# Attention over 16 batches: the large heads' probabilities transposed on VectorE and moved by transfers, five weights reloaded per batch

## The chip, the core and the metric

The kernel runs on one core of a Trainium2 chip. The metric is the device time of one execution in microseconds (us). The engines are TensorE (PE, with its weight loads PEld), VectorE (DVE), ScalarE (ACT), GpSimd (POOL) and SyncE (SP), which here only issues transfers.

## The reference, cut to what matters

Four cross-attention layers follow each other for 16 batches. `x` is (16, 100, 256) and the context is (16, 361, 256). All are float32, and every layer has 16 heads. Layers 0 and 3 have heads of 16 columns ("small heads"), layers 1 and 2 have heads of 64 columns ("large heads").

```python
# layer 0: layer norm of query and context, heads of 16, then a feed-forward block
scores = einsum('bqhd,bkhd->bhqk', Q, K) / sqrt(16)
x = residual + softmax(scores) @ V @ wo + bo
x = x + gelu(layer_norm(x) @ w1 + b1) @ w2 + b2
# layer 1: root-mean-square norm of the query, heads of 64, no scale
x = x + softmax(q @ k.T) @ v @ wo
# layer 2: heads of 64, rotary embedding of q and k, scale 1/8, mask, layer norm at the end
scores = where(mask, rope(q) @ rope(k).T / 8, -1e9)
x = layer_norm(x + softmax(scores) @ v @ Wo)
# layer 3: layer norms, heads of 16, biases, residual
```

The weighted sum of one head contracts over the 361 keys, so the probabilities, which leave the softmax with the 100 queries on the partitions, must be turned so that the keys lie on the partitions.

## The kernel before

The program is written out as a list of works (`Plan.add`, L263): each names the engines that can run it, its reads, writes and buffers. `Plan.order` (L304) replays the list with estimated durations, chooses an engine and a buffer slot for each work, and gives the final order of instructions on every engine. The ranks in `ORDER` (`lag`, `place`, `ends`) are constants that shift this choice. On the chip every engine then runs its instructions in that order, and waits on semaphores where a work reads what another engine or a transfer writes. Two batches at a time are in flight, with buffers of their own (`p = b % 2`); the loop over the 16 batches is `for b in range(B): batch(b)` (L1443).

All weights are kept on the chip: twelve slabs of 128x2048 float32 (1 MB each) are loaded once at the start (`load_slab`). After that SP issues only the batch's context, query rows and mask, and the store of the result.

An attention layer (`Attention`, L904) goes through four units (`unit`, L922), each of four heads. For one unit:

- `scores` (L933): TensorE multiplies queries and keys into one PSUM bank per head, 361 keys in two parts of 181 and 180. The large heads take 64 rows of the array each, so that two heads run side by side.
- `exponential` (L975): VectorE negates the scores and takes their maximum in one pass (L991); with a mask, in layer 2, it takes the minimum with the cap (L985) and then the maximum (L988). ScalarE takes the exponential with the sum of the row (L997).
- `softmax` (L953): VectorE inverts the sums (L961), GpSimd divides (L968).
- `transposed` (L1011): TensorE transposes the probabilities of two heads by 12 instructions (L1032): for each head and each of three chunks of 128 keys, 64 queries and 36 queries at two places of the array. The results lie in PSUM, and ScalarE or VectorE copies them to `pT` in three copies per unit (`copied`, L711 and L713). There are two `pT` buffers.
- `weighted` (L1052): TensorE multiplies `v` and `pT` (through `on_columns`, L830), chunk by chunk of the keys.

`values` (L1300) computes `v` of half of the large heads at a time, with the keys of chunk `j` on the partitions. `rotated` (L874) applies the rotary embedding of layer 2: VectorE swaps neighbouring rows out of PSUM (`stream_shuffle`, L885), GpSimd multiplies by the sine (L889), VectorE multiplies PSUM by the cosine (L892), and GpSimd adds both (L897). `feed_forward` (L1339) uses `w1` and `w2`, `project_out_T` (L1124) an output weight. `by_parity` (L1202) spreads the small heads' queries over two copies, on VectorE.

TensorE runs in tiling modes (`row64` for transposes and large scores, `row32` for small scores, `col32` for all projections and weighted sums), and the plan groups works of one mode.

Of the kernel before, what the change touches and what calls it, by code (L numbers as in the profile page):

```python
# [17 lines left out]
P = 128  # L18
# [6 lines left out]
SKP = NKC * KP  # L25
BIG = 3.0e38
# [5 lines left out]
for _name, _w in (  # L32
# [10 lines left out]

SLABS = (
# [12 lines left out]
    "lag": 281400, "pull": 6.35, "window": 0,  # L57
    "keep": {None: 4180, "row64": 280, "row32": 710, "col64": 3610, "col32": 5250},
    "run": {None: 3260, "row64": 33260, "row32": 18740, "col64": 46890, "col32": 300},
    "batch": (-614500, -19500, 0, 0, 0, 0, 0, 0, 0, 0, 0, 0, 0, 0, 6000, -863500),  # L60
    "place": [
        100 * k for k in (
        1530, 2179, 1302, -155, -3146, -3119, -1447, -50, 2198, -4316, -4647, -2582, -7311,
        -6990, -6791, -975, -6218, -4297, -1712, -7295, -4489, -3822, -7130, -4520, -2986,
        -5107, -1814, 2539, -585, 44, -2295, -3865, -3674, -5144, -5622, -10071, -9468, -6347,
        -6509, -5109, -6468, -10008, -6583, -10112, -6656, -7056, -6274, -9553, -10961, -12648,
        -6592, -6491, -10074, -11842, -5012, -7475, -5864, -2138, -2644, -2757, -1752, -1661,
        -3175, -1806, -475, 295, -1528, -1314, -130, -2596, -3455, -3510, -486, 819, -960, -351,
        -262, -1091, -2095, 773, 352, 609, -2745, -1077, -4127, -3906, 1115, -1980, -1044, 199,
        1113, -2251, -559, -4303, 204, 507, -7028, -6650, -4569, -6483, -2121, -3493, -985,  # L70
        -4030, 928, 291, -3776, -3852, -4367, -2262, -3068, -1405, 3055, -1796, -1471, -2884,
        -3509, -3745, -408, -473, -4075, -5224, -5147, -1610, -3815, -3333, -4064, -6731, -5900,
        -7478, -6211, -2778, -3243, -2860, 346, 2670, -1934, 358, -4143, -3642, -2093, -2165,
        -529, 13, -685, -1077, -415, 5064, -896, -533, -6410, 8, -1286, 795, -1181, 3287, 2325,
        1250, 437, 2327, 2459, -1757, -1578, -5694, -990, 2513, 7808, 7794, 4228, 183, 3326,
        3721, 2104, 3855, 1016, 3932, -5255, -932, -801, -1656, 458, -71, 3547, -2879, -7942,
        1183, -679, -3284, -3147, -4837, -4906, -3658, -1029, -5460, -1795, -2290, -3716, -633,
        -1243, 250, 3042, 115, 3644, 209, 517, 802, 3561, 2033, 8348, 2938, -2370, -768, 91,
        -3053, -3682, 21, -551, -703, 11, -1354, -76, -6811, -5354, -5457, -3261, -4456, -5041,
        -4118, -7857, -5743, -9610, -9289, -7014, -6103, -6155, -5974, -3208, -5827, -5655,  # L80
        -3748, -6019, 1222, -6204, 1169, 1555, 804, 4287, 847, 1540, 2681, 4086, 3349, 8301,
        3405, 2300, 1930, -158, 2379, 3910, 4211, 3253, -272, -266, -2428, -1347, 2024, 88,
        -3112, -7985, -3868, 994, 1277, -1300, -464, -390, 2333, 3472, 2811, 3971, 4406, 6487,
        7550, 8667, 4711, 4737, 1877, 3779, 2319, 8022, 4465, 4476, 4993, 5707, 6778, 4543,
        5848, 4450, 5898, 5280, 5713, 2599, 4430, 8324, 4133, 8528, 6706, 596, 2298, -498, -905,
        1966, -4295, -1105, -3795, -5564, -1315, 1532, -3363, -2789, -552, 18, -3105, -6266,
        -10045, 1320, -6270, -4428, -689, -4740, -3580, 963, -5363, -2314, 1942, 5363, 3756,
        3169, 735, -4085, 2025, 1750, 1971, 2138, 2974, 3519, 5203, 5507, -452, 3042, -190, 412,
        -928, -229, 3162, -526, 895, -1352, -1376, -3942, -3984, -379, -7134, -2812, 551, -6423,
        -2341, -2152, -3333, 1507, -1188, 1764, 4650, 1708, -78, 1087, 3668, 2857, -1320, -858,  # L90
        -553, -1310, -4001, -416, -2796, -2804, -3944, -3808, -3234, -2595, -5780, -8117, -7507,
        -10136, -9612, -9238, -7690, -3249, -4884, -5928, -7611, -6301, -4692, -3495, -11110,
        -9091, -6761, -5493, -6295, -1317, -740, 731, -2244, -69, -536, 1225, -1389, -3686,
        -3052, 1470, -6939, -3363, -3396, -8455, -10700, -13129, -12689, -11245, -7208, -10167,
        -10536, -5830, -7870, -7456, -6041, -4659, -7272, -4839, -3132, -1617, -5559, -2862,
        1514, 625, -188, 1018, -3554, -7159, -3278, -5544, -4708, -2643, -3131, -6058, -6394,
        1652, -6383, 298, -1138, -636, 2469, 408, -1417, 3200, 3186, 3478, 1178, 3587, 3199,
        6766, 4361, -6638, -2795, -3377, -7601, -7151, -544, 106, 696, 3907, 4138, 174, -2346,
        -2919, -5554, -4166, -6125, -7266, -5804, -4121, -1761, -2439, -2442, -6500, -2289,
        -5069, -2101, -1548, -4952, -9599, -7022, -7908, -8951, -3814, -1275, 1254, 521, 1148,  # L100
        2417, 2197, 5182, 1520, 1334, -2249, -1420, -3655, 2699, 1623, 5275, 3648, 4868, 2758,
        2532, -689, 507, -519, 767, 6121, 2545, 1546, 1364, 5831, 5011, 3375, 4931, 2510, 1069,
        -2819, -2364, -1352, 736, 211, 7491, 5251, 3010, 3340, -1837, -316, -4152, -1590, -7796,
        -2636, -2985, -4463, -3344, -3607, -3647, -175, 99, 2885, 1406, -3051,
        )
    ],
    "ends": {
        0: (
            -360, -553, -1511, 2397, 964, 789, -725, 912, 2373, -371, 41, 464, 1613, 1142, 2683,
            1305, 1591, 1084, 1716, 523, 2216, 90, -1353, -388, -1656, -1072, -274, -339, -11,  # L110
            155, 632, -171, 502, -673, -1637, -182, 1897, 672, 1857, -596, -378, -333, 1238,
            2379, 469, 1904, -164, 63, -794, 573, 808, -1509, -1850, -1626, -1597, -3151, -3544,
            -2672, -900, -1650, -798, -2350, -1910, -1679, -1847, -698, -2383, -2743, -5180,
            -4612, -2344, -2016, -1852, -3270, -1884, 112, 362, -992, -1005, 724, 1778, 650,
            2305, 599, 2425, 619, 1458, 3273, 1790, 4855, 2263, 3341, 5414, 1727, 1515, 3046,
            1719, 1836, 3007, 3679, 2096, 2898, 5452, 3383, 5487, 2059, 2757, 3025, 3143, 6789,
            5244, 6917, 4771, 5135, 4386, 3985, 5106, 4688, 5087, 4942, 4236, 3046, 2670, 2706,
            3503, 2091, 1847, 3076, 2014, 1388, 1104, 1622, 656, -58, -699, -1176, 358, 1608,
            650, 1589, 2114, 1883, 2341, 2921, 2511, 3381, 3691, 4413, 3140, 4228, 2483, 3948,
            2043, 2066, 931, 1432, 1360, 1782, -86, -18, 837, -930, -270, -363, 814, 2353, 1627,  # L120
            643, -38, -161, -146, -1206, -375, -3069, -315, -3728, -3105, -3361, -2754, -3800,
            -1483, -3606, -4088, -5311, -4059, -5705, -6399, -5862, -6911, -5959, -5318, -4142,
            -5855, -4077, -6440, -6281, -5759, -5040, -4004, -6200, -4200, -5136, -4332, -4595,
            -3567, -4424, -2153, -3404, -4608, -3125, -3018, -1565, -4138, -1906, -3823, -2916,
            -4261, -4211, -4430, -4353, -4078, -4346, -2581, -1226, -3347, -414, -1217, -70,
            352, -362, 2766, 1590, 2947, 76, 1035, 1343, 2115, 230, 1068, 914, 987, 299, 1055,
            684, -333, -908, -1103, 180, 966, 2428, 1138, 3173, 2381, 3194, 2268, 2281, 4818,
            2345, 3968, 2898, 2699, 4290, 3602, 3022, 1639, 2723, 1823, 1069, 1598, 615, 1470,
            1948, 1732, 1430, 1545, 3316, 3001, 2864, 1194, 2011, 1984, 1999, 2991, 940, 1758,
            492, 994, -419, 2734, 3609, -90, 190, 731, 2958, 562, 689, 1347, 969, -80, 453, 154,  # L130
            56, -1037, 348, -1744, 43, 860, -1679, 219, -1277, -405, -1163, 609, -392, -842,
            664, -1860, -2046, -2459, -1830, -3185, -2962, -3331, -4173, -2284, -952, -420,
            -2511, -2702, -1827, 984, -629, -2108, -2626, -2178, 617, -343, -442, -299, 2765,
            1451, 1872, 3147, 1723, 1384, 657, 2253, 2961, 4622, 1312, 1265, 3200, 448, 335,
            974, 1119, 332, 1507, -455, -919, 902, 3211, 2790, 2410, 3753, 1212, 3920, 2793,
# [57 lines left out]
        ),  # L193
    },
}

class Buf:
# [209 lines left out]
def tile_xattn_layers(  # L409
# [147 lines left out]
    for i in (2, 3, 6):  # L557
        load_slab(i)
# [939 lines left out]
```

## Time and profile before

| | |
|---|---|
| median of 2 runs | 1936.38 us (1935.73 to 1937.03) |
| span of the profiled execution | 1935.2 us |
| mean granted TensorE clock | 0.993 |
| TensorE busy | 1914.6 us (99%) |
| VectorE busy | 1294.5 us (67%) |
| ScalarE busy | 1170.2 us (60%) |
| GpSimd busy | 1045.9 us (54%) |
| TensorE transposes of the probabilities (L1032) | 6144, 240.8 us busy |
| transfers | 29.94 MB, 15 GB/s over the span |

The profile is of one execution, and its span is 1.2 us below the median of the runs. "Busy" is the time in which at least one instruction of the group was running. TensorE's instructions overlap, so a group's mean duration is far above the time that one more instruction adds. The mean of the transposes is 226 ns, while 24 of them take 0.89 us from the first start to the next work's start. The granted clock is the share of full speed that TensorE was given.

### The profile page before, as it was taken

The numbers are of one execution on the slowest core, as the hardware profiler recorded it, in microseconds if no ns is written. First come the engines' busy times: TensorE is split into PE (matmuls) and PEld (weight loads), VectorE is DVE, ScalarE is ACT, GpSimd is POOL, SyncE is SP. The second block draws the span as 40 slices with busy tenths as digits, with TensorE's granted clock in tenths as the row PEclk, the third lists the DMA queues.
The fourth block names the chain that finished last, engine by engine and source line by source line (L and its number), as shares of the span: only waits on it lengthen the run. The fifth ranks groups of instructions, "written<-read, shape, count | busy, mean of one in ns | idle before, by whom it ended". The sixth has DMA issues, their size and how long they took to land.

```text
span 1935.2 us, 99776 instructions
## 1 busy us (share of the span) xinstructions
PE 1914.6 (99%) x43881; PEld 1268.0 (66%) x43881; DVE 1294.5 (67%) x4502; ACT 1170.2 (60%) x3418; POOL 1045.9 (54%) x1682
## 2 busy tenths in 40 slices
PE   8999999999999999999999999999999999999997
PEld 4667666575766757667575675766657576575766
DVE  5556676766667666666666676667676667765776
ACT  4646556575665746657566565665657566575645
POOL 5355465555556555555645555556555555654564
PEclk9999999999999999999999999999999999999997
DMA  7000000000000000000000000000000000000000
GB/s 305 3 3 14 5 12 8 3 14 5 12 8 3 14 5 12 8 3 15 5 14 6 11 9 3 14 5 12 8 3 14 6 12 8 3 15 5 3 3 7
DMA packets 14730, 29.94 MB, mean 15 GB/s; under 512 B 3362, under 2 KB 12376, under 8 KB 12888
## 3 DMA queue, kind: packets, MB, share of 16 engines
q1 hardware_dynamic: 14296, 23.56, 3.8%
q8 instruction: 344, 5.64, 1.2%
q14 instruction: 90, 0.74, 0.1%
HBM read 21.92 MB, written 1.64 MB: 12 GB/s over the span
## 4 chain that ended last, share of the span: by engine, by line
PE 97%; DVE 1%; POOL 1%; ACT 0%; issue 0%; DMA 0%; SPq 0%; POOLq 0%; DVEq 0%; ACTq 0%
PE ps L830 70%; PE ps L936 14%; PE ps L1032 11%; PE ps L771 1%; PE ps L858 1%; PE ps L813 0%; ACT prob L997 0%; DMA slab<-slabs_dram 0%; DVE prob L991 0%; PE ps L616 0%; PE ps L665 0%; POOL prob L968 0%; DVE pT L713 0%; DVE prob L985 0%; POOL kT L897 0%
## 5 line engine op out<-in xcount | busy, mean ns | idle before, releaser
L968 POOL TENSOR_SCALAR prob<-prob,two 100x361 f32<-100x361 f32 x1024 | 566.2, 571 | 551.6 <-DVE two L961 335.2
L997 ACT ACTIVATE prob<-prob,two 100x361 f32<-100x361 f32 x1024 | 602.0, 592 | 138.6 <-DVE prob L991 87.2
L991 DVE TENSOR_SCALAR_CACHE_REDUCE prob<-ps 100x361 f32<-100x361 f32 x768 | 372.3, 530 | 143.7 <-PE ps L936 126.7
L830 PE MATMUL ps<-slab,cT 128*32 128x512 f32 (+1 forms) x3072 | 367.0, 595 | 0.0
L830 PE MATMUL ps<-cT,slab 128*32 128x361 f32 x4096 | 346.0, 468 | 0.0
L936 PE MATMUL ps<-kT,qT 32*100 32x181 f32 (+3 forms) x4096 | 303.3, 328 | 2.9 <-DVE qT L1204 1.4
L711 ACT COPY pT<-ps 128x384 f32<-128x384 f32 (+1 forms) x521 | 231.1, 492 | 93.4 <-PE ps L1032 77.4
L936 PEld LDWEIGHTS ps<-kT,qT 32*100 32x100 f32 (+1 forms) x4096 | 228.1, 164 | 74.8 <-issue 30.8
L1032 PEld LDWEIGHTS ps<-ident,prob 36*128 36x128 f32 (+1 forms) x6144 | 215.3, 140 | 85.1 <-POOL prob L968 62.8
L1032 PE MATMUL ps<-ident,prob 64*128 64x64 f32 (+1 forms) x6144 | 240.8, 227 | 1.5 <-ACT pT L711 0.8
L713 DVE COPY pT<-ps 128x384 f32<-128x384 f32 (+1 forms) x247 | 137.4, 573 | 130.9 <-PE ps L1032 128.7
L711 ACT COPY v<-ps 128x512 f32<-128x512 f32 (+1 forms) x119 | 69.7, 586 | 245.6 <-PE ps L830 161.8
L830 PEld LDWEIGHTS ps<-cT,slab 128*32 128x32 f32 x4096 | 123.1, 109 | 134.7 <-issue 122.4
L997 ACT ACTIVATION_READ_ACCUMULATOR prob<-prob,two 100x1 f32 x1024 | 194.0, 189 | 0.0
L889 POOL TENSOR_TENSOR sw<-sw,rot 128x361 f32<-128x361 f32 x128 | 105.3, 824 | 135.6 <-DVE sw L885 110.2
L830 PEld LDWEIGHTS ps<-slab,cT 128*32 128x32 f32 (+1 forms) x3072 | 85.3, 107 | 139.2 <-issue 127.3
L985 DVE TENSOR_TENSOR prob<-ps,cap 100x361 f32<-100x361 f32 x256 | 125.5, 527 | 62.6 <-PE ps L936 37.9
L830 PE MATMUL ps<-pT,v 128*32 128x100 f32 (+1 forms) x6144 | 155.3, 250 | 0.3 <-ACT pT L711 0.3
L830 PEld LDWEIGHTS ps<-pT,v 128*32 128x32 f32 (+1 forms) x6144 | 136.0, 110 | 22.7 <-issue 13.2
L897 POOL TENSOR_TENSOR kT<-kT,sw 128x361 f32<-128x361 f32 x128 | 122.5, 959 | 5.7
L988 DVE TENSOR_REDUCE two<-prob 100x1 f32<-100x361 f32 x256 | 125.6, 517 | 0.0
L830 PE MATMUL ps<-xT,slab 128*32 128x100 f32 x5120 | 124.1, 252 | 1.1 <-ACT xT L791 1.1
(105 smaller groups left out, 2329.6 us busy)
## 6 DMA issues: line engine op xcount, KB each, us to landing
slab<-slabs_dram SPq DMA_DIRECT2D x11, 1024.0 KB
ctxr<-ctx_dram SPq DMA_DIRECT2D x16, 256.0 KB
ctxr<-ctx_dram SPq DMA_DIRECT2D x16, 105.0 KB
x<-x_dram SPq DMA_DIRECT2D x16, 100.0 KB
out_dram<-x SPq DMA_DIRECT2D x16, 100.0 KB
slab<-slabs_dram SPq DMA_DIRECT2D x2, 512.0 KB
mask<-mask_dram SPq DMA_DIRECT2D x16, 45.1 KB
rows<-rowvecs_dram SPq DMA_DIRECT2D x1, 640.0 KB
```

The costliest lines, as they stand in the source:

```text
L711: nc.scalar.copy(dst(), src())
L713: nc.vector.tensor_copy(dst(), src())
L830: nc.tensor.matmul(out_f(at + t, at + t1), lhsT=lhsT[:, t:t1], rhs=rhs, start=start, stop=stop, tile_position=(0, at + t),)
L889: nc.gpsimd.tensor_tensor(a, a, wide(sin()), ALU.mult)
L897: nc.gpsimd.tensor_tensor(dst_f(dst.ap), dst_f(dst.ap), sw.ap[:, :n], ALU.add)
L936: nc.tensor.matmul(banks[h].ap[:S, k0:k1], lhsT=self.q_of(h), rhs=self.k_of(h)[:, k0:k1], start=(k0 == 0), stop=(k1 == SK), skip_group_che ...
L968: nc.gpsimd.tensor_scalar(p.ap[:S, :SK], p.ap[:S, :SK], rsum.ap[:S, j : j + 1], 1.0, ALU.mult, ALU.mult,)
L985: nc.vector.tensor_tensor(p(), bank.ap[:S, :SK], self.cap.ap[:S, :], ALU.min)
L988: nc.vector.tensor_reduce(neg_max.ap[:S, 0:1], p(), AX.X, ALU.max, negate=True)
L991: nc.vector.tensor_scalar(p(), bank.ap[:S, :SK], -1.0, None, ALU.mult, ALU.min, accum_out=neg_max.ap[:S, 0:1],)
L997: nc.scalar.activation(p(), p(), AF.Exp, bias=neg_max.ap[:S, 0:1], scale=1.0 if masked else -1.0, accum_out=sums.ap[:S, j : j + 1],)
L1032: nc.tensor.transpose(out[:, c, :], probs[h].ap[q0:q1, c * KP : (c + 1) * KP], ident[q0:q1, q0:q1],)
```

## The change

For the large heads alone, TensorE no longer transposes the probabilities. Queries are laid out in four blocks of 32 columns, of which 25 hold queries and seven stay zero (`QN`, `BLK`, `spread`, `split`), so that the scores of a large head have 128 rows. The new `exchanged` replaces `transposed`: for each pair of heads one VectorE instruction transposes all 32x32 blocks of the probabilities (128x768) into `blocks`. The keys of a block are then on the 32 partitions of the query block's quadrant. Sixteen transfers per unit, issued by SP, take each quadrant's blocks to the quadrant of `pT` that the weighted sum needs, in runs of 1536 bytes per partition. There are three `blocks` buffers and three `pT` buffers; the small heads still go through `transposed` and share `pT`. `values` puts the keys on the partitions in the matching order, and the weighted sum reads its 100 query columns as four runs of 25.

To make room, five weights (`STREAMED`) are no longer kept: `stream` loads each of them again for each batch into one of two `ring` buffers. The large heads' `v` has three buffers in place of two for each parity of the batch.

In `rotated`, the product with the cosine moves to GpSimd, after a copy out of PSUM by ScalarE or VectorE. `by_parity` can also run on ScalarE. Two memsets of `qT` are added at the start. All constants of `ORDER` are different, so the order of the works differs on every engine.

```diff
-        "prob": slots_of("prob", 8, [P, SKP]),
-        "pT": slots_of("pT", 2, [P, 4, NKC, S]),
+        "prob": slots_of("prob", 4, [P, 2, SKP]),
+        "blocks": slots_of("blocks", 3, [P, 4, NKC, 4 * BLK]),
+        "pT": slots_of("pT", 3, [P, NKC * NQ * 4 * BLK]),
+
+        "v": slots_of("v", 3, [P, NKC, 512]),
+        "ring": slots_of("ring", 2, [P, 2048]),
...
     for p in range(2):
+        nc.gpsimd.memset(slots[f"qT{p}"][0], 0.0)
...
+    def stream(name, b, begun):
+
+        t = plan.buf("ring", f"{name}_{b}")
+        i = SLABS.index((name,))
+
+        def issue(_):
+            nc.sync.dma_start(out=t.ap, in_=slabs[i])
+
+        return t, plan.add([("SP", 450.0, 7000.0)], issue, writes=[t], begun=begun)
...
         def times_cos(_):
-            nc.vector.tensor_tensor(
-                shaped(dst_f(dst.ap)), shaped(ps.ap[:, :n]), wide(cos()), ALU.mult
-            )
+            a = into()
+            nc.gpsimd.tensor_tensor(a, a, wide(cos()), ALU.mult)
...
         plan.add(on_dve(n + 20), swap, reads=[ps], writes=[sw])
         plan.add(on_pool(2.3 * n), times_sin, reads=[sw, rot], writes=[sw])
-        plan.add(on_dve(n), times_cos, reads=[ps, rot], writes=[dst])
+        copied(into, lambda: shaped(ps.ap[:, :n]), n, [ps], [dst])
+        plan.add(on_pool(2.5 * n), times_cos, reads=[dst, rot], writes=[dst])
         plan.add(on_pool(2.5 * n), both, reads=[sw, dst], writes=[dst])
...
+            self.rows = P if hd == 64 else S
...
-                                banks[h].ap[:S, k0:k1], lhsT=self.q_of(h),
+                                banks[h].ap[: self.rows, k0:k1], lhsT=self.q_of(h),
...
+            turned = self.exchanged if hd == 64 else self.transposed
+            self.weighted(i, groups, heads, turned(probs, heads, f"{name}_{i}"))
...
+        def exchanged(self, probs, heads, name):
+
+
+            blocks, pT = plan.buf("blocks", f"{name}_blocks"), plan.buf("pT", f"{name}_pT")
+            made = []
+            for u, (prob, parts) in enumerate(probs):
+                made.append(plan.buf(None, f"{name}_made{u}"))
+
+                def transpose(_, u=u, prob=prob):
+                    to = blocks.ap[:, :, :, 2 * u * BLK : 2 * (u + 1) * BLK].rearrange(
+                        "p b c (h q) -> p h (b c) q", h=2
+                    )
+                    nc.vector.transpose(to, prob.ap.rearrange("p h (b q) -> p h b q", q=BLK))
+
+                plan.add(
+                    [("DVE", 870.0, 955.0)], transpose, reads=[prob, *parts], writes=[made[u]],
+                    takes=[blocks],
+                )
+
+            def p_of(h, c, n):
+                a = pT.ap.rearrange("p (j c h q) -> p j c h q", c=NKC, j=NQ, h=4)
+                return a[:n, :, c, heads.index(h), :QN]
+
+            def move(_):
+                for j in range(NQ):
+                    for b in range(4):
+                        n = NKC * 4 * BLK
+                        nc.sync.dma_start(
+                            out=pT.ap[b * BLK : (b + 1) * BLK, j * n : (j + 1) * n],
+                            in_=blocks.ap[j * BLK : (j + 1) * BLK, b].rearrange("p c n -> p (c n)"),
+                        )
+
+            plan.add([("SP", 5600.0, 8000.0)], move, reads=[blocks, *made], writes=[pT])
+            return pT, p_of
...
+        o_buf, _ = stream(wo, b, begun=[att.first[2]])
+        return project_out_T(att.oT, 8, wo, o_buf, resid, p, f"L{L}_x_{b}"), att
+
+    def feed_forward(b, xt, gate):
         p = b % 2
+        w1_buf, loaded = stream("L0_xattn_w1", b, begun=[gate])
+        w2_buf, _ = stream("L0_xattn_w2", b, begun=[loaded])
...
+        q_buf, _ = stream("L2_xattn_Wq", b, begun=[att.first[3]])
```

## The prediction

> **What bounds the kernel now.** I read the page first: busy time by engine, then the chain that ended last.
>
> ```profile
> PE 1914.6 (99%) x43881; PEld 1268.0 (66%) x43881; DVE 1294.5 (67%) x4502; ACT 1170.2 (60%) x3418; POOL 1045.9 (54%) x1682
> PE 97%; DVE 1%; POOL 1%; ACT 0%; issue 0%; DMA 0%; SPq 0%; POOLq 0%; DVEq 0%; ACTq 0%
> q1 hardware_dynamic: 14296, 23.56, 3.8%
> ```
>
> TensorE is busy for 99% of the span and holds 97% of the chain; the next engine, VectorE, is at 67%, and the transfers are almost idle. Work taken off TensorE is time, as long as nothing new makes it wait. Next the groups by shape, and the chain in order of time for one stretch (start, duration, what):
>
> ```profile
> L1032 PE MATMUL ps<-ident,prob 64*128 64x64 f32 x3072 | 240.8, 226 | 1.5 <-ACT pT L711 0.8 <-POOL prob L968 0.2
> L885 DVE STREAM_SHUFFLE sw<-ps 128x361 f32<-128x361 f32 x128 | 73.5, 575 | 0.6 <-issue 0.4
> L885 DVE STREAM_SHUFFLE sw<-ps 128x400 f32<-128x400 f32 x32 | 19.6, 614 | 0.0
> L892 DVE TENSOR_TENSOR kT<-ps,rot 128x361 f32<-128x361 f32 x128 | 66.9, 524 | 9.8 <-PE ps L830 9.1 <-PE ps L813 0.7
> 908.12 0.89 PE ps L1032 x23
> ```
>
> One unit of four heads costs TensorE 0.89 us for its transposes, first start to the next work's start. Last, the timeline of the transfer queue (start, duration, instruction), and two stretches of the table by windows (length, busy times PE to POOL, granted clock, DMA share, GB/s):
>
> ```profile
> 21.16 4.38 SPq L517 DMA_DIRECT2D slab<-slabs_dram  x5
> 300.42 0.30 SPq L494 DMA_DIRECT2D x<-x_dram  x1
> 331.51 0.30 SPq L1436 DMA_DIRECT2D out_dram<-x  x1
> 32.00:36.00 4.00, 4.00 (x104) 2.87 (x100) 1.74 (x4) 2.96 (x8) 3.84 (x7) 1.00 1.02 426
> 1900.00:1908.00 8.00, 4.04 (x78) 3.02 (x82) 6.14 (x28) 5.47 (x18) 4.47 (x8) 0.70 0.00 0
> ```
>
> An ordinary issue takes 0.30 us of the queue, five large ones in a row 0.88 us each. With all transfer engines busy at 426 GB/s, TensorE was busy throughout at full clock, so transfers as such do not slow it. Where it waits, the clock falls (0.70 at the end).
>
> **The change part by part.**
>
> *Transposes off TensorE.* 2 large layers x 16 batches x 4 units = 128 units; in the listing 3072 of 6144 transposes are gone. 128 x 0.89 = 113.9 us by the chain; starts to next starts over all 6144 (222.3 us) give 111.2, half of the group's busy time 120.4. I take **-111**. The other TensorE work keeps its count. Changes between tiling modes go from 823 to 790, which I count as nothing.
>
> *Wider scores.* Large heads load 128 columns of queries instead of 100. Weight loads of the same two passes took 90 ns with 9 columns and 109 with 32, 0.83 ns a column: 28 columns are 23 ns, over 2048 loads, two at a time, 24 us if nothing hid it. Loads overlap the 181-column matmul before (329 ns): I take 0, bounds 0 to 24. The weighted sum reads the same 100 columns in runs of 25; broken runs have no row. Rows of 100 unbroken columns lie between 249 and 255 ns; 2% of its 140 us is 3. I take 0.
>
> *VectorE.* Added: 256 block transposes of 128x768. No row; nearest are the shuffles: 39 more elements cost 39 ns, so 614 + 368 x 1.0 = 982 ns; by proportion 1223 ns. I take 0.98: +251 us (upper end 313). Lower end: 768 elements at half the shuffle's slope plus its 214 ns, 0.60 us. Removed by the listing: 109 copies to pT (62 us), the 160 products of L892 (85), 89 query scalings (28), and some copies shift between engines. VectorE ends near 1294.5 + 251 - 183 = 1362 us, 74% of 1840. ScalarE loses 275 copies to pT (136 us) and gains 80 kT copies (36), 89 query scalings (31) and smaller ones: about 1155. GpSimd takes over the products: 128 x 0.82 to 0.96 plus 32 x 1.04, +147, near 1193 us, 65%. None reaches TensorE's sum, so these cost nothing while it is the bound; without that cover the largest is 68 us net on VectorE.
>
> *The exchange.* Per unit SP issues 16 transfers of 32 rows x 1536 bytes. At 0.30 + 0.01 us each they need 5.0 us, 128 x 5.0 = 640 us of the queue. The output store issued at 331.51 had its last packet near 333.0: 1.5 us. Each transfer waits for the completion of the eighth before it; eight issues take 2.5 us, so that wait is covered. Packets: the queue's 14296 took 3.8% of 16 x 1935.2, 82 ns each; 512 / 16 x 82 = 2.6 us per exchange, under the issue time. Price of one exchange: 15 x 0.31 + 1.5 = **6.2 us**; upper end, at 0.88 us each, 14.7.
>
> The Trainium skill's DMA: Bandwidth & Descriptors, section Bandwidth, speaks against this: batch to 1 MiB, since a transfer of 64 KB takes 0.95 us alone. One after the other, 16 would take 15.2 us by it and 128 units 1946 us, an estimate from that page with no gain left. The rows here show packets of several transfers overlapping, and the issue as the limit.
>
> *Is it hidden?* Behind the exchange waits the weighted sum at L1065, and behind it all of TensorE's queue. From the scores of a unit to its weighted sum, the chain by rows: first maximum 0.61, four exponentials 0.58 apart plus the accumulator read 2.5, reciprocal 0.16, two divisions 1.11, block transpose 0.98, exchange 6.2: 11.6 us; masked layer, with two VectorE passes a head, 13.4. In the changed program's listing I summed the TensorE work that stands between the two, each work at its start-to-start time of before: median 21.6 us, a tenth below 18.5. So 5 to 8 us are left for queueing, in the steady batches: cost 0. Only the last batch's last four units have 15.7, 11.2, 7.3 and 3.7 us; the last waits 13.4 - 3.7, **+10** (0 to 20: at clock 0.63 the waits and the works around them double). More counters are waited for: 885 wait instructions on TensorE for 428; those were under 0.5% of the chain, so at most 10 us for 457 more; I take **+4**.
>
> *Weights.* 80 loads of 1 MB replace five kept slabs. The shortest stretch of TensorE work between the last use of a ring slot and the first use of its next content is 12.0 us; issue 0.9 plus 1.05 MB at 305 GB/s, the first slice's rate, is 4.4. Hidden. If an SP wait on a slot held up the exchange behind it, that would eat the 5 to 8 us above. In all some 200 MB move, at 305 GB/s 0.66 ms, a third of the span. Two 1.06 us memsets of qT at the start lie in GpSimd's idle 2.2 us before the first normalization: 0.
>
> Sum: 1935.2 - 111 + 10 + 4 = 1838 us of span; the median of the runs stands 1.2 above the span: **1840**.
>
> The clock is the term most easily missed. In the last 35 us TensorE waited 0.2 to 1.4 us at a time and the same scores took 1.54 us instead of 0.87. The Trainium skill's TensorE: Matmul & The Clock Gate, Part 1, has the clock halve only after an idle window of about 3.4 us; by that rule short waits would cost just themselves, while the rows show it low among shorter ones. The sum uses the row.
>
> **The rivals.**
>
> *Half given back (the waits return in the steady state).* For: the exchange adds 6.2 us to a chain that ran without it, three slots each for blocks and pT hold units in flight, two transfers of before were issued behind others in 1.46 and 1.91 us, and VectorE at 1.22 us a transpose would be at 77%. Against: 18.5 us of cover. If half of the 128 units waited 0.8 us, 51 us: 1891; range 1865 to 1897.
>
> *The queue becomes the pace.* Mechanism: SP serves the 2048 exchange transfers in order, each with its own issue. At the slabs' 0.88 us they take 1802, 80 loads 70, the batches' own loads 16 x 1.8 = 29, together 1901 us: no change. It decides from 0.92 us per transfer (1884 + 99 = 1983 us), and at 1.0 us the time is 2048 + 99 = **2147**, slower. For: the run of slabs, and 1.46 us behind a mask. Against: every x load and store at 0.30 with fewer issues but more rows each.
>
> *The transposes do not leave the bound:* VectorE becomes it from (1840 - 1111) / 256 = 2.85 us per block transpose; nearest row 0.61. Little speaks for it.
>
> That the change fails to do what it says is excluded for the counts, by the listing.
>
> **How the numbers follow.** Forecast (1815 to 1865): 0.66. Half given back: 0.18. Between, within 2% of before (1897.7 to 1975.1, about what a measurement of this kernel can tell from no change): 0.05. Slower, by the queue's pace or waits of over 1.2 us per unit: 0.10; faster than 1815: 0.01. Range: low end 1935.2 - 120.4 + 1.2 = 1816, without tail or waits; it goes up through the second case to 1895, leaving out under 0.2. Faster by over 2%: 0.66 + 0.18 + 0.01 = 0.85.
>
> **What would show it.** Right: the transposes' group at about 111 us, TensorE at 98% or more of a span near 1838, SP issues near 0.31 us within an exchange, block transposes near 0.98 us, waits of the weighted sum on pT only in the last 30 us. Wrong: waits of the weighted sum on transfers spread over all batches, a clock below 0.97, or exchange issues of 0.5 us and more.

## The result, and the profile after

The changed kernel takes **2538.12 us** (median of two runs, 2537.66 to 2538.58) against 1936.38 us before: a ratio of 1.310, 95% interval 1.307 to 1.314. It is 602 us slower, where 1840 us was forecast. The profiled execution has a span of 2536.7 us and a mean granted clock of 0.885.

First the page of the changed kernel: busy time by engine, the granted clock in 40 slices, the transfer queue, the chain, four groups, and the issues of the exchange (count, KB each, median us to landing).

```profile
PE 2033.8 (80%) x40809; PEld 1302.3 (51%) x40809; DVE 1348.8 (53%) x4394; ACT 1177.5 (46%) x3402; POOL 1191.9 (47%) x1840
PEclk9988898889989889888899888988889889899885
...
q1 hardware_dynamic: 123400, 203.01, 27.4%
...
PE 6%; SPq 5%; DMA 1%; DVE 1%; issue 1%; ACT 1%; POOL 0%; DVEq 0%; ACTq 0%
...
L955 PE MATMUL ps<-pT,v 128*32 128x100 f32 (+1 forms) x6144 | 228.3, 316 | 421.1 <-DMA pT<-blocks 403.8
...
L1152 DVE STREAM_TRANSPOSE blocks<-prob 128x768 f32<-128x768 f32 x256 | 242.4, 963 | 99.6 <-DMA pT<-blocks 84.2
...
L1199 PE MATMUL ps<-ident,prob 64*128 64x64 f32 (+1 forms) x3072 | 137.1, 238 | 6.2 <-POOL prob L1098 4.0
...
pT<-blocks SPq DMA_DIRECT2D x2048, 48.0 KB, 2.0
```

TensorE fell from 99% to 80% of the span: it stands idle for 503 us, 404 of them before weighted sums whose probabilities have not landed (the last number of the L955 line). No engine took its place: VectorE, ScalarE and GpSimd are at 46 to 53%. The transfer engines are at 27%, so bytes are not short either. The clock is low in slices all over the span. The chain's shares add up to 15%; it breaks off early and says little here. So the next two views are TensorE's waits (us in total, times, longest) and the queue itself (start, duration, instruction):

```profile
PE ps L955 <- DMA pT<-blocks: 403.8, 101, 10.7
PE ps L938 <- DVE rT L1322: 34.2, 7, 6.7
```

```profile
909.96 11.17 SPq L1167 DMA_DIRECT2D pT<-blocks  x16
921.17 0.58 SPq L631 DMA_DIRECT2D ring<-slabs_dram  x1
921.92 22.42 SPq L1167 DMA_DIRECT2D pT<-blocks  x32
944.45 0.53 SPq L605 DMA_DIRECT2D mask<-mask_dram  x1
945.14 11.22 SPq L1167 DMA_DIRECT2D pT<-blocks  x16
...
1006.50 11.25 SPq L1167 DMA_DIRECT2D pT<-blocks  x16
1017.79 1.06 SPq L631 DMA_DIRECT2D ring<-slabs_dram  x2
1018.96 0.32 SPq L1647 DMA_DIRECT2D out_dram<-x  x1
1019.45 37.37 SPq L1167 DMA_DIRECT2D pT<-blocks  x48
```

Sixteen issues take 11.2 us of SP, 0.70 us each from start to start on the mean (median duration 0.589 us). The forecast had 5.0 us. And they are not spread out: in this stretch four exchanges follow each other almost without a break, 909.96 to 956.36 and again 1006.50 to 1056.82, and between them SP has 50 us without any. So an exchange waits for those before it. Over the whole run, 8.3 us pass on the mean from the end of a unit's second block transpose to its first issue (6.5 in the middle, over 5 for 77 of the 128); in 1006 of these 1058 us SP is inside earlier exchanges (worked out from the trace). Two stretches of the table by windows (length, busy PE to POOL, clock, DMA share, GB/s), the first ahead of such a bunch, the second in it:

```profile
985.00:1015.00 30.00, 29.88 (x708) 21.67 (x703) 24.22 (x97) 22.95 (x74) 17.14 (x30) 1.00 0.08 20
1020.00:1065.00 45.00, 31.34 (x700) 20.54 (x693) 16.14 (x60) 17.00 (x50) 18.50 (x28) 0.85 0.33 101
```

Between the bunches TensorE runs as before. In a bunch it is busy for 70% of the time, at clock 0.85.

### The profile page after: what moved, and what is told of

Same layout as the page of the kernel before. It is cut to its first block, busy times and chain, and to the rows that moved or that the text cites. A ratio compares the mean times of both kernels' runs of the same rounds, so it can differ in the third digit from the quotient of the medians.

```text
span 2536.7 us, 97201 instructions
## 1 busy us (share of the span) xinstructions
PE 2033.8 (80%) x40809; PEld 1302.3 (51%) x40809; DVE 1348.8 (53%) x4394; ACT 1177.5 (46%) x3402; POOL 1191.9 (47%) x1840
## 5 line engine op out<-in xcount | busy, mean ns | idle before, releaser
L1098 POOL TENSOR_SCALAR prob<-prob,two 100x361 f32<-100x361 f32 (+1 forms) x1024 | 568.2, 571 | 809.9 <-DVE two L1091 736.9
L1126 ACT ACTIVATE prob<-prob,two 100x361 f32<-100x361 f32 (+1 forms) x1024 | 602.6, 592 | 290.0 <-DVE prob L1120 195.9
L955 PE MATMUL ps<-pT,v 128*32 128x100 f32 (+1 forms) x6144 | 228.3, 316 | 421.1 <-DMA pT<-blocks 403.8
L1120 DVE TENSOR_SCALAR_CACHE_REDUCE prob<-ps 100x361 f32<-100x361 f32 (+1 forms) x768 | 373.2, 527 | 153.5 <-PE ps L1067 141.1
L955 PEld LDWEIGHTS ps<-pT,v 128*32 128x32 f32 (+1 forms) x6144 | 194.4, 141 | 488.5 <-issue 432.7
L955 PE MATMUL ps<-cT,slab 128*32 128x361 f32 x4096 | 369.4, 490 | 0.3 <-issue 0.3
L1067 PEld LDWEIGHTS ps<-kT,qT 64*128 64x128 f32 (+1 forms) x4096 | 258.6, 192 | 102.3 <-issue 39.9
L1152 DVE STREAM_TRANSPOSE blocks<-prob 128x768 f32<-128x768 f32 x256 | 242.4, 963 | 99.6 <-DMA pT<-blocks 84.2
L955 PEld LDWEIGHTS ps<-cT,slab 128*32 128x32 f32 x4096 | 126.6, 114 | 141.3 <-issue 120.3
L1126 ACT ACTIVATION_READ_ACCUMULATOR prob<-prob,two 100x1 f32 (+1 forms) x1024 | 194.0, 189 | 0.0
L836 ACT COPY pT<-ps 128x384 f32<-128x384 f32 (+1 forms) x246 | 109.0, 492 | 168.6 <-PE ps L1199 117.4
L1022 POOL TENSOR_TENSOR kT<-kT,rot 128x361 f32<-128x361 f32 x128 | 123.1, 962 | 119.1 <-ACT kT L836 106.6
L1199 PEld LDWEIGHTS ps<-ident,prob 64*128 64x128 f32 (+1 forms) x3072 | 119.0, 150 | 44.9 <-issue 28.1
L1114 DVE TENSOR_TENSOR prob<-ps,cap 128x361 f32<-128x361 f32 x256 | 123.1, 521 | 32.5 <-PE ps L1067 30.9
```

Source lines behind the costliest of these rows:

```text
L836: nc.scalar.copy(dst(), src())
L955: nc.tensor.matmul(out_f(at + t, at + t1), lhsT=lhsT[:, t:t1], rhs=rhs, start=start, stop=stop, tile_position=(0, at + t),)
L1022: nc.gpsimd.tensor_tensor(a, a, wide(cos()), ALU.mult)
L1067: nc.tensor.matmul(banks[h].ap[: self.rows, k0:k1], lhsT=self.q_of(h), rhs=self.k_of(h)[:, k0:k1], start=(k0 == 0), stop=(k1 == SK), skip_ ...
L1098: nc.gpsimd.tensor_scalar(a, a, rsum.ap[:n, j : j + 1], 1.0, ALU.mult, ALU.mult)
L1114: nc.vector.tensor_tensor(p(), bank.ap[:n, :SK], self.cap.ap[:n], ALU.min)
```

## The experiments

Theory: SP, which issues one transfer after the other, is too slow for the exchanges of a bunch, because an issue costs twice what was forecast. Rivals: the runs of 1536 bytes or their packets; only the weighted sums wait, each for its own exchange; the reloads of the weights in the same queue; other parts of the change. Every experiment is one run; the kernel before took 1935.7 to 1938.1 us beside them.

**m1_issues: the price of an issue alone.** A small program issues eight transfers of each shape and computes nothing. It replaces the whole kernel.

```python
inside("sq_32x384", 384, 32, 0, 32, nc.sync)    # on the chip to the next quadrant
...
inside("sq_128x384", 384, 128, 0, 0, nc.sync)   # on the chip, 128 rows
...
load("ld_100x256", 100)                         # from device memory
...
store(32)                                       # to device memory
inside("aq_32x384", 384, 32, 0, 32, nc.scalar)  # on ScalarE's queue
```

> A kernel that only issues transfers, eight in a row of each shape, and computes nothing of the reference. Theory 'issue': SP needs 0.59 us to issue one transfer of 32 rows from one place of the on-chip memory to another, also when nothing else runs; then the rows of 32x384 within the memory show 0.55 to 0.62 us, and 32x96 the same, because bytes do not count. Rival 'contention': the 0.59 us came from the other engines and the weight loads of the full kernel; then the same shape shows 0.27 to 0.35 us here. The other shapes tell what the issue depends on: if on both ends lying on the chip, loads and stores of 32 rows show 0.30 us and 100 rows within the memory show 0.6; if on the number of transfer engines that a shape is spread over, 34 rows show less than 32 rows, and loads of 32 and 128 rows more than loads of 100.

It took 81.24 us. Its queue (start, duration of the group, instruction):

```profile
2.14 5.34 SPq L28 DMA_DIRECT2D sq_32x<-src  x8
7.53 5.04 SPq L28 DMA_DIRECT2D sq_32x_same<-src  x8
...
17.70 5.16 SPq L28 DMA_DIRECT2D sq_128x<-src  x8
...
34.25 6.77 SPq L28 DMA_DIRECT2D sq_32x<-src  x8
...
53.00 2.62 SPq L36 DMA_DIRECT2D ld_32x<-ctx_dram  x5
55.67 3.04 SPq L36 DMA_DIRECT2D ld_100x<-ctx_dram  x8
...
62.97 3.68 SPq L40 DMA_DIRECT2D out_dram<-src  x8
```

One issue takes 0.63 to 0.67 us from start to start where both ends lie on the chip (5.04 / 8 and 5.34 / 8; median durations 0.589 and 0.609, the second beside ScalarE's issues). A store takes 0.46 us (3.68 / 8), a load of 32 rows 0.52 (2.62 / 5) and one of 100 rows 0.38 (3.04 / 8); the median durations of the loads are 0.41 us for 32 rows and 0.34 for 100. On the chip the median duration is 0.57 to 0.61 us for 16, 32, 34 and 128 rows of up to 1536 bytes, and 0.71 and 0.73 for 40 and 100 rows. Bytes count once there are enough of them: eight copies of 32 rows of 6144 bytes took 6.77 us, with a median of 0.87. No other work competes here, so the price is not one of contention.

**e1_half_runs: half the bytes.**

```diff
-  in_=blocks.ap[j * BLK : (j + 1) * BLK, b]   # runs of 1536 bytes
+  in_= ... half of it                         # runs of 768 bytes, still 16 transfers
```

> The changed kernel with each of the 16 transfers of an exchange cut to runs of 768 bytes in place of 1536; half of the probabilities is left behind. Theory 'issue': the time per issue stays at 0.59 us, the exchange near 11.2 us, and the kernel within 2% of 2538 us. Rival 'bytes': the transfers' data is what is slow (a packet of 1536 bytes took 0.095 us); then issues fall toward 0.35 us and the time below 2200 us.

2500.5 us, issues still 0.589 us, 10.97 us per exchange. Half the bytes bring 38 us of 602: bytes and packets are not the cause.

**e4_no_transfers, e2_eight, e7_twelve: 0, 8 and 12 transfers per exchange.** In the first the weighted sums of the large heads read a kept slab; in the others the last two or the last one of the four key blocks is left out.

```diff
-  for b in range(4):
+  for b in range(2):      # e2_eight; range(3) in e7_twelve; no transfer at all in e4_no_transfers
```

> Left out: all 2048 exchange transfers; the weighted sums of the large heads read a kept weight slab in place of the transposed probabilities. Everything else (wider scores, 256 block transposes, runs of 25 rows, weights reloaded per batch, the new order) stays. Theory 'the exchange's place on SP's queue is the whole loss': with 1431 us of issues gone the loss goes too, 1840 to 1910 us, TensorE's clock 0.98 or more, waits for the ring of weights (116 us in the kernel whose weighted sums did not wait) under 25 us. Rival 'the new order, the reloads of weights or the block transposes cost much by themselves': 2000 us or more.

> The changed kernel with 8 transfers per exchange in place of 16, each as before; half of the probabilities is left behind. Theory 'issue': the exchange takes 5.6 us of SP and lands 1.4 us later, 7.0 in all, about what the prediction had put (6.2); TensorE's waits on transfers fall from 404 us to under 40, the clock rises above 0.97, and the time is 1830 to 1900 us. Rival 'something else in the order' (lanes, weight loads, block transposes): above 2200 us.

> Left out: the last of the four 32-key blocks of every quarter of the queries, so 12 transfers per exchange instead of 16; its rows of the transposed tile are zero. Between 8 transfers (1915 us) and 16 (2538 us). Theory 'pace of the queue with a point from which it decides': 12 issues take 12 x 0.66 = 7.9 us (by 10.97 and 11.18 us for 16), landing 2 us later; the queue is over its cover already, but only by part of what 16 are: 2050 to 2280 us, less than the middle of the two (2226) if the loss begins between 8 and 12, exchange issues still 0.58 to 0.60 us each. Rival 'loss in proportion to the transfers': 2226 us, within 30.

| transfers per exchange | SP per exchange, mean us | time, us |
|---|---|---|
| 0 (e4_no_transfers) | none | 1903.1 |
| 8 (e2_eight) | 5.72 | 1915.2 |
| 12 (e7_twelve) | 8.46 | 2199.3 |
| 16 (changed kernel) | 11.18 | 2538.1 |

The second column is worked out from the trace, first issue's start to last issue's end. From 12 to 16 transfers it grows by 2.72 us, times 128 exchanges 348 us, and the time grows by 339: in this step a microsecond of issuing costs about a microsecond of the kernel. From 8 to 12 it is 351 us of issuing and 284 of time. If the price were the same there, the first 67 us, 0.5 us per exchange, were free, and the queue decides from about 6.2 us per exchange. By itself the run with twelve does not refute a loss in proportion between 8 and 16: 2199 lies within the 30 us that the rival gave itself around 2226. But from 0 to 8 transfers only 12 us were lost, so there is a point below which the exchange is hidden.

Two reasons for the point can be read in the traces. In the run without transfers the pairs of block transposes end 5.8 us apart (median of the 127 distances, mean 13.9; the same 5.8 in the run with eight), because in each batch they come in bunches with pauses of some 50 us. A queue that needs more per exchange falls behind in the bunch. And one exchange has little room even when it starts at once: in the run with eight, TensorE comes to the weighted sum 11.6 us after the second block transpose in the middle, and after at most 8.4 us in the shortest tenth. With 2.0 us to landing, an exchange is late there from a stay of 6.4 us on SP, and in the middle of the units from 9.6. Both reasons give nearly the same point, so the runs with 8, 12 and 16 do not separate them.

The run without transfers puts the rest of the change at 1903 us, 1.7% under before. Its weighted sums do not wait for the softmax and the block transposes either; in the run with eight they do, and it takes 1915 us, a little over the 1900 expected of it. So the rest lies between 1903 and 1915. Here are the busy times by engine of the run without transfers, and after them TensorE's waits on the exchange in the run with eight (us in total, times, longest):

```profile
PE 1842.6 (97%) x40809; PEld 1191.2 (63%) x40809; DVE 1345.6 (71%) x4394; ACT 1171.3 (62%) x3402; POOL 1190.8 (63%) x1840
```

```profile
PE ps L957 <- DMA pT<-blocks: 7.8, 3, 4.4
```

Eight transfers leave 8 us of waits, sixteen 404.

**e3_no_wait: the transfers stay, nobody on TensorE needs them.** The weighted sums of the large heads read a kept slab.

```diff
-  a = pT.ap.rearrange(...)
+  a = slab_t[5][:, :1536].rearrange(...)
```

> The changed kernel with all transfers, but the large heads' weighted sums read a kept weight in place of the moved probabilities, so that TensorE does not wait for the exchange. Theory 'late, not too many': SP has 1431 us of exchanges and some 100 us of other issues, less than the span, so without the wait the kernel takes 1840 to 1950 us at a clock above 0.97. Rival 'the queue is the pace': slots of blocks come free too late, VectorE waits for them and everything behind it, and the time stays above 2200 us.

2370.1 us: only 168 us come back. TensorE's waits and VectorE's:

```profile
PE ps L955 <- DMA ring<-slabs_dram: 116.2, 9, 16.2
PE ps L955 <- ACT pT L836: 56.5, 23, 4.6
PE ps L1067 <- DVE prob L1120: 54.0, 7, 10.1
```

```profile
DVE blocks L1152 <- DMA pT<-blocks: 205.4, 36, 9.6
```

The late queue makes itself felt through whatever stands behind it: reloads of weights that come after the exchanges in SP's order, and slots of `blocks` and `pT` that come free late, so that VectorE waits and TensorE after it. The theory that the weighted sums alone are late, which expected 1840 to 1950 us, falls.

**e8_no_reloads: no weights behind the exchanges.**

```diff
+  if b < 1:
       nc.sync.dma_start(out=t.ap, in_=slabs[i])
```

> Left out: the weights' reloads after the first batch (75 of 80 one-MB loads), so later batches compute with whichever weights lie in the two ring slots. The 16 transfers per exchange stay. In the changed kernel SP stood 272 us before reloads that wait for TensorE to finish with a slot, and the exchanges queued behind. Theory 'the sixteen issues set the pace and standing behind others' waits adds to it': the loss of 600 us falls by 100 to 300 us, to 2240 to 2440 us. Rival 'standing behind the reloads is most of it': under 2100 us. Rival 'it only moves the wait to the next instruction': 2480 us or more.

2466.3 us, between what the theory and the last rival gave: 72 us less. SP's waits before reloads (289 us in the changed kernel) turned into longer waits before exchanges: 386 and 276 us for two of VectorE's results, where the changed kernel has 297 and 115. The reloads are a small part.

**e9_every_other: half the exchanges, each as long as before.**

```diff
+  kept = self.turn                    # 1, 0, 1, 0 ...
-  for j in range(NQ):
+  for j in range(NQ if kept else 0):
```

> Left out: all 16 transfers of every other exchange (64 of 128); the weighted sums of those units read a kept weight slab. So as many transfers as with 8 per exchange (1915 us), but each exchange that is left still takes its 11.2 us. Without transfers the pairs of block transposes end 5.8 us apart in the middle of their distances, in bunches, with a pause of some 50 us in every eight. Theory 'SP's pace in a bunch decides': 11.2 us fall on two units, 11.6 us, so the queue just keeps up: 1915 to 2000 us. Rival 'one exchange of 11.2 + 2 us outlasts the work between its scores and its weighted sum': half of the exchanges are as late as before and half of the 600 us stays, 2150 to 2300 us.

2097.5 us, between the two again, though it has as many transfers as e2_eight (1915). The excess over 1903 us is 3.0 us for each exchange that is left; with all of them it is 5.0. A line of its queue and TensorE's waits on the exchange:

```profile
919.67 22.58 SPq L1170 DMA_DIRECT2D pT<-blocks  x32
```

```profile
PE ps L955 <- DMA pT<-blocks: 141.0, 36, 9.1
```

The two exchanges in one piece look like a queue that has fallen behind, but it has not. Their block transposes end at 919.6 and 929.9, and their first issues start at 919.7 and 930.8. Over the run an exchange starts 0.1 us (median) after its block transposes, where the changed kernel has 6.5. So here the queue keeps up, and TensorE still waits 141 us: one exchange of 11.4 + 2.0 us alone outlasts the 11.6 us that it has in the middle. At 3.0 us each, 128 such exchanges would cost 389 of the 635 us (an estimate). The loss therefore has two parts, the stay of the single exchange and the queueing in a bunch; both come from the price of the issues, and the runs do not give the exact split.

**e13_from_slab and e14_from_hbm: the price alone.** Both keep the 16 transfers, their sizes, destinations and places in the queue, but read constant data, one from a slab on the chip, the other the same weights from device memory.

```diff
-  in_=blocks.ap[j * BLK : (j + 1) * BLK, b]...
+  in_=slab_t[5][j * BLK : (j + 1) * BLK, b * n : (b + 1) * n]   # e13_from_slab
+  in_=slabs[5, j * BLK : (j + 1) * BLK, b * n : (b + 1) * n]    # e14_from_hbm
```

> Left out: the data of the exchange. The 16 transfers per exchange have the changed kernel's places in the queue, their sizes, their number and their destination, but read a kept weight slab on the chip, so they no longer wait for the block transposes, only for the queue and for a free slot of the transposed tile. It is the counterpart of the next run, with which alone it is compared. Both theories: issues of 0.59 us, exchanges of about 11.2 us, 2150 to 2500 us.

> As the run before it, with the same 16 transfers of 32 rows of 1536 bytes, the same order and the same waits, but the source is the same weights in device memory. Theory 'the price of an issue whose ends both lie on the chip': 32-row loads took 0.41 to 0.43 us to issue, 16 take 6.9 us, little more than the 5.8 us between two exchanges of a bunch: 1910 to 2060 us, at least 200 us under its counterpart. Rival 'the number of transfers, of their waits or their bytes': within 40 us of its counterpart.

2327.6 us from the chip, **2065.0 us** from device memory, 5 us over the expected end. The issues have a median of 0.589 and 0.419 us, an exchange takes SP 11.34 and 9.00 us. The difference, 2.34 us x 128 = 300 us, comes out as 263 us of time. TensorE's waits on the exchange in the one and the other:

```profile
PE ps L955 <- DMA pT<-slab: 305.6, 67, 12.9
```

```profile
PE ps L955 <- DMA pT<-slabs_dram: 111.7, 35, 7.5
```

Number, bytes, destinations and order are equal, and the median landing is 2.0 us in both, so the place of the source and the price of issuing from there make the difference: the price theory holds. It is not all, though: at the price of loads the exchange still costs 162 us over the run without transfers, and TensorE waits 112 us for it. Both runs are to be compared only with each other: their transfers do not wait for the block transposes.

**e10_two_queues: half the issues on ScalarE's queue.**

```diff
-  nc.sync.dma_start(
+  (nc.sync if j < 2 else nc.scalar).dma_start(
```

> Nothing left out: of the 16 transfers of an exchange 8 are issued by SP and 8 by ScalarE's queue, at the same time. ScalarE, 1177 us busy, takes 1024 issues at 0.66 to 0.70 us on top, 675 to 715 us, and they stand in its order among the exponentials. Theory 'the price is that of the issuing engine': each issue is still about 0.59 us on either queue, an exchange is through after about 5.6 us, but ScalarE at some 10 us per unit in a bunch becomes what is late: 2050 to 2350 us, with waits on ScalarE's results in place of those on the transfers. Rival 'both queues share the price': issues of 1.2 us while both run, exchanges of 11 us as before, 2500 us or more.

2477.1 us, worse than expected. Issues have a median of 0.592 us on SP's queue and 0.603 on ScalarE's while both run, so the price belongs to the queue that issues. But ScalarE's exponentials now stand behind its issues:

```profile
ACT prob L1126 <- DMA pT<-blocks: 367.3, 57, 9.8
```

**e6_bounce: five issues instead of sixteen.** One store of the whole `blocks` tile to device memory, then four loads of 32 partitions.

```diff
+  nc.sync.dma_start(out=far, in_=blocks.ap.rearrange("p b c n -> p (b c n)"))
+  for b in range(4):
+      nc.sync.dma_start(out=pT.ap[b * BLK : (b + 1) * BLK, :]..., in_=far[:, b * n : (b + 1) * n]...)
```

> Nothing left out: the same exchange by way of device memory, one store of the whole blocks tile (786 KB) and four loads of 32 partitions with 4 x 1536 bytes each, 5 issues per unit instead of 16. Theory 'the number of issues with both ends on the chip is the price': store about 0.35 us and loads about 0.42 us each to issue (100-row store 0.374, 32-row load 0.409 measured alone), but the loads wait for the store to land (about 3 to 4 us), so about 1 + 3.5 + 2 + 2.5 = 8 to 9 us from transposes to landing, SP's stay per exchange about 6 us of which 2 us are issues: 1890 to 1990 us. Rival 'the wait on the queue costs as the issues did': the store's landing holds SP as long as 16 issues, 2200 us or more.

2153.2 us, near the rival. Its waits on SP's queue, two stretches of that queue, and the loads (count, KB each, median us to landing):

```profile
SPq L1170 <- DMA bounce<-blocks: 642.0, 128, 11.0
```

```profile
941.77 0.33 SPq L1168 DMA_DIRECT2D bounce<-blocks  x1
945.14 1.95 SPq L1170 DMA_DIRECT2D pT<-bounce  x4
```

```profile
pT<-bounce SPq DMA_DIRECT2D x512, 192.0 KB, 3.7
```

The five issues take 2.3 us, but SP stands 5.0 us (642 / 128) for the store to land before it may issue the loads. It is held 7.3 us per exchange. By the line between eight and twelve transfers that would give some 2080 us (an estimate); the loads also land later, 3.7 us after their issue instead of 2.0. It is the fastest version that computes everything with transfers, and slower than before.

**e11_replanned and e12_bounce_planned: another order.** The planner gets the measured durations, and the ranks in `ORDER` are chosen anew for them. In the second, store and loads are works of their own.

```diff
-  plan.add([("SP", 5600.0, 8000.0)], move, reads=[blocks, *made], writes=[pT])
+  plan.add([("SP", 10600.0, 13200.0)], move, reads=[blocks, *made], writes=[pT])   # e11_replanned
```

> Nothing left out: all 16 transfers per exchange, the same works and buffers, but the planner counts 10.6 us of SP and 13.2 us to landing per exchange in place of 5.6 and 8.0, and the ranks of the works are chosen anew for these numbers, so that exchanges stand further apart. Theory 'bunches of exchanges make the queue the pace, though it has room on the average (128 x 11.2 = 1431 us)': the same issues in another order, 2150 to 2350 us, the waits on the exchange well under the 404 us of the changed kernel. Rival 'the stay of one exchange, not the order, makes the loss': 2450 us or more.

> Nothing left out: the exchange by way of device memory (one store, four loads), with the store and the loads as two works of their own, so that SP may issue other transfers while a store lands, and with ranks of the works chosen for the times of the version before it (store 0.4 us and 5.4 to landing, four loads 1.9 and 4.4). Theory 'SP's stay per exchange in a bunch, now about 2.3 us instead of 7.5, is what counts': 1930 to 2010 us. Rival 'the longer way to landing, some 10 us from the transposes, outlasts the cover whatever the order': 2080 us or more, near the 2153 of the version before it.

2414.5 and 2206.7 us: the first lies between its two expectations, the second is slower than the bounce in the old order and refutes what the theory expected of it. In e11_replanned TensorE waits on the exchange for 133 us instead of 404, but it is still idle for 402 us, in many small waits for other results. In e12_bounce_planned the waits on the exchange are 63 of 240 us of idle time. These ranks were chosen in a short search, so the runs do not show what the best order would give. They do not support the idea that the planner's numbers alone made the loss.

## Why the prediction was wrong, by its own steps

**The step that failed: the price of the exchange.** The prediction took the 0.30 us of the x loads and output stores for an issue, and argued that they have more rows than the exchange. But those rows have one end in device memory, and the exchange has both on the chip. There an issue costs 0.59 us, 0.70 from start to start on the mean. Part of the gap is not the ends: the same 32-row transfers from device memory took 0.42 us (e14_from_hbm), and the trace of before had loads at that price, as this one of the context:

```profile
282.67 0.42 SPq L493 DMA_DIRECT2D ctxr<-ctx_dram  x1
```

So 0.12 us were lost by choosing the cheapest row, and 0.17 by the ends. The stay also holds waits that the prediction took as covered. It says rightly that each transfer waits for the eighth before it; but where that is a reload of 1 MB, SP stands (the changed kernel; us in total, times, longest):

```profile
SPq L1167 <- DMA ring<-slabs_dram: 33.4, 24, 4.7
```

Landing took 2.0 us for the 1.5 read off a store; the Trainium skill's SBUF — State Buffer, section The DMA setup-cost knee, states a fixed cost of about 2 us for every transfer, mostly completion, and the 2.0 us row agrees. One exchange is 11.2 + 2.0 = 13.2 us instead of 6.2, within the bound of 14.7.

**The second: whether the exchange is hidden, and the point from which the queue decides.** The rival of the queue named one right mechanism and put its point at 0.92 us per transfer, by dividing the whole time by all transfers. In bunches only about 5.8 us lie between two exchanges; by the runs with 8 and 12 the point is about 6.2 / 16 = 0.39 us. At the price assumed, 5.0 us, the forecast would have stood clear of it; at the price found it was nearly twice over. The cover itself was right: from the end of a unit's scores to its weighted sum the run with eight has 22.5 us in the middle and 18.7 in the shortest tenth, for 21.6 and 18.5. But the chain ahead of the exchange was too short. The sum gave it 5.4 us (11.6 - 6.2), and 7.2 in the masked layer; measured, from the end of the scores to the second block transpose, it is 10.2 us in the middle. Its terms are durations one after the other, without any waiting for engines that also serve other work. That leaves the exchange 11.6 us in the middle: room for the 6.2 assumed, not for 13.2. And the cover was counted for one unit by itself, and does not see that exchanges queue behind each other: with four in a row, the last starts 3 x (11.2 - 5.8) = 16 us late (an estimate; the longest tenth in the trace is over 17). The 1802 us that the rival feared for the whole queue never came up: SP's exchanges add up to 1431 us, and in the rest it waits, in order, for outputs, slots and the next bunch. The rule of the Trainium skill's DMA: Bandwidth & Descriptors that was weighed and set aside, 0.95 us for a transfer of 64 KB and 15.2 for an exchange, came nearer to the measured 13.2 us than the row that was chosen. That is luck: the page measured it for loads from device memory issued by GpSimd, as busy time of the transfer engines and not as issue time. Its 1946 us for 128 units was 592 us off, since it too spreads the cost over the batch.

**The clock.** Between the changed kernel and the run without transfers lie 635.4 us of span: 444 us more idle time on TensorE (502.9 less 58.7), and 191 us more busy time for the same 40809 matmuls (2033.8 less 1842.6), at a clock of 0.885 instead of 0.987. Each two microseconds of waiting went with nearly another one. Of the idle time, 335 us lie in 60 waits of over 3.4 us, long enough for the rule that the prediction quoted from the Trainium skill's TensorE: Matmul & The Clock Gate, Part 1. Other runs show that shorter waits go with a low clock too: e11_replanned has 402 us idle, only 138 of them in waits of over 3.4 us, and a clock of 0.912; e3_no_wait has 405 us idle, 307 of them in such waits, and 0.906. In the tail of the kernel before, the clock was halved three times with no wait of TensorE over 1.0 us in the 8 us ahead of it (worked out from the trace). So the single long window does not account for the clock here, and the prediction did well to take the row.

**The rest of the sum** can be judged by the run without transfers, 1901.3 us of span against the 1838 of the sum. The transposes that left TensorE were worth 98 us instead of 111 (222.3 to 124.4 us, starts to next starts; those that stayed run at 40 ns instead of 36). All scores together cost 12 us more (280.6 to 292.5); 7 of them lie in the widened ones (172.6 to 179.9), for which 0 was taken and 24 was the bound. TensorE's idle time grew by 38 us, 27 of them in small waits between 100 and 1750 us, where 14 were allowed for tail and wait instructions together. The rest of the 63 us is slower starts in the other matmuls: some 20 us, where idle time that lies inside the first two terms is counted once. So even without the exchange the gain was 1.7% and not 5%.

**Right:** the block transposes (0.963 us for 0.98), VectorE at 1349 us (1362), ScalarE at 1178 (1155), GpSimd at 1192 (1193), the instruction counts, the cover, that transfer engines are not short, and that none of the computing engines becomes the bound. What was named as showing the forecast wrong, waits spread over all batches, a clock under 0.97 and issues of 0.5 us and more, is what the profile shows.

## What to carry to other kernels

Price an issue by a row with the same two ends: one of a load does not hold for a copy within the chip. Compare a queue's stay with the distance of its jobs inside a bunch, not with the mean over the run, and with the room that one job has. Remember that an in-order queue hands its lateness to all that stands behind it. Where work is moved off the bound onto transfers, measure first the version without the transfers: here it was 33 us faster than the kernel before, and that was the most there was to win.

## What the runs showed of the hardware that was not expected

- An issue on SP's queue took 0.589 us (median) for the exchange's copies within the chip. Alone it took 0.57 to 0.61 us for 16, 32, 34 and 128 rows, 0.71 and 0.73 for 40 and 100 rows, and 0.87 for rows of 6144 bytes, against 0.33 to 0.41 us for loads and 0.35 to 0.42 us for stores. ScalarE's queue has nearly the same price (0.60 us). Why both ends on the chip cost more was not tried.
- About one exchange issue in 16 (125 of 2048) took some 1.4 us, at no fixed place in the exchange. They and 42 us of waits inside the exchanges, most of them for a reload to land, raise the mean of a stay to 11.2 us, where sixteen median starts of 0.633 us would give 10.1. The cause of the long issues stays open.
- A store of 786 KB to device memory held SP for 5.0 us on the mean before its data could be read back, as long as eight issues within the chip.
